# Layer 1 of a two-layer graph attention: weighted sums of h in 128x32 tiles, W applied to the sums, and scores from dot products on VectorE

## The chip, the cores and the metric

The kernel runs on one core of a Trainium2 chip. The metric is the device time of one execution in microseconds (us), the median of several runs; a profile of one execution shows what each engine does. TensorE multiplies matrices (PE in the profile; PEld are its weight loads), VectorE is DVE, ScalarE is ACT, GpSimd is POOL, and SP issues all DMAs here. Everything is float32 except masks.

## What is computed

There are 8 graphs (batches) of 2048 nodes with 256 features, and one adjacency matrix for all. Layer 0 is attention with four heads in which each chunk of 256 keys has a softmax of its own; then come a projection, a residual and two layer norms. Its result is h. Layer 1 is what the change touches:

```python
def _L1_gnn_ref(h, adj, W, a):
    Wh = jnp.einsum('bnf,fo->bno', h, W)
    a1 = a[:Fout, 0]
    a2 = a[Fout:, 0]
    s_i = Wh @ a1
    s_j = Wh @ a2
    e = jax.nn.leaky_relu(s_i[:, :, None] + s_j[:, None, :], negative_slope=LEAKY_ALPHA)   # 0.2
    mask = (adj > 0) | jnp.eye(N, dtype=bool)
    e = jnp.where(mask[None, :, :], e, -jnp.inf)
    attention = jax.nn.softmax(e, axis=-1)
    h_prime = jnp.einsum('bij,bjo->bio', attention, Wh)
    return jax.nn.elu(h_prime)

x = _layernorm(x + _L0_gnn_ref(x, adj, ...), axis=-1)      # this x is h
x = _layernorm(x + _L1_gnn_ref(x, adj, L1_gnn_W, L1_gnn_a), axis=-1)
```

h comes out of a layer norm without scale and offset, so its features sum to zero in each row.

## The kernel before

Work is cut into blocks of 512 queries (ib, four to a batch) and tiles of 128 keys. The order of instructions on every engine is that of the program: it is written out by hand in **beats**. A beat is one tile of 128 keys of layer 0 for one block of queries; a batch has 64 beats, all eight have 512, and a tail of shorter beats finishes layer 1.

In each beat layer 0 multiplies q and k into scores (L886, two heads side by side in 64x128 tiles), clips and masks them on VectorE (L897), exponentiates on ScalarE (L901), and for the pair of key tiles before multiplies with v and with ones (L955). This last is done in 128x32 tiles: four instructions, one per head, write four groups of 32 PSUM partitions, and each streams 512 columns; such a group of four is called a quad here. A float32 matmul is two instructions, so the profile counts each twice. The results are copied by ScalarE (un L963, ds L969), the sums go through DRAM (dc, rd, r), and VectorE and GpSimd scale and add them to ctxT (L990, L991).

A finished block of layer 0 goes through `fin` (L345): projection po (L361), residual, two layer norms, h stored to DRAM (L380), then h transposed on TensorE (pt, L387), copied (L388) and stored as hT_d (L392).

Layer 1 of a batch runs beside layer 0 of the next one. `prelude` (L479) loads hT in blocks, makes Wh and the two scores per node as columns of one product with W and two appended columns (pw, L402, copied at L403), lays s_j out as a row (sj_row), and finds for each query the largest s_j among its neighbours (`half_max`, L442, VectorE). Out of that `less_max` makes two rows per block, ab: s_i less the row maximum, and 0.2 s_i less the row maximum. The last batch has `last_prelude` (L521), in part in the tail.

A **step** of layer 1 is one tile of 128 keys for one block: 16 steps a block, 512 in all. Up to 1.5 start in a beat on average (1.3 in the last batch of layer 0, one in the tail). A step writes one tile w of 128x512, from a ring of five:

- `low` (L718, ScalarE): 0.2 s_j added to the second row of ab;
- `leaky` (L722, VectorE, one beat later): s_j added to the first row, and the larger of both;
- `edges` (L727, VectorE, middle of that beat): the smaller of this and a mask of 0 or -128;
- `weights` (L731, ScalarE, next beat): exp; and L740 (GpSimd) adds the tile to acc, for the row sums;
- `product` (L750, TensorE, end of that beat): four matmuls, each with 128 queries of w as weights and 256 columns of Wh streaming, into us (two PSUM banks).

In the last batch the row sum is a column of ones beside Wh (L765, 257 columns). After the sixteenth step ScalarE copies us to hx (L777); `fin1` (L592) sums acc over partitions with one-column matmuls (pr, L601), takes reciprocals, scales hx (L605), applies elu, adds h, normalizes and stores. `fin1_last` (L617) does this in smaller pieces.

The loops that issue all this are `begin_beat`, `middle_of_beat` and `end_beat` (L820 to L860) and the loop over beats (L904). Generators for side work (`fins`, `ahead`) advance once a beat, at its end, so a `yield` means one beat. Buffers come from pools named by their number of buffers; PSUM has ps_s (scores, two), ps_u (us, one) and ps_m (all else, two).

Of the kernel before, what the change touches and what calls it, by code (L numbers as in the profile page):

```python
# [14 lines left out]
ALU = mybir.AluOpType  # L15
# [13 lines left out]
def tile_adj_attention__then__gat(  # L29
# [16 lines left out]
    W: bass.AP,  # L46
    a: bass.AP,
# [43 lines left out]
    five = ctx.enter_context(tc.tile_pool(name="five", bufs=5))  # L91
# [26 lines left out]
    def xT_tile(b, ib, name):  # L118
        t = four.tile([P, KC, IB], F32, tag="xT", name=f"xT_{name}{b}_{ib}")
        nc.sync.dma_start(out=t, in_=xT[b, :, ts(ib, IB)].rearrange("(k p) n -> p k n", p=P))  # L120
        return t
# [104 lines left out]
    W_aug = const.tile([P, KC, F + 2], F32, name="W_aug")  # L226
    nc.sync.dma_start(out=W_aug[:, :, 0:F], in_=W.rearrange("(k p) o -> p k o", p=P))
    a_bc = []
    for n in range(2):
        t = one.tile([P, F], F32, tag=("hx", "ex")[n], name=f"a_bc{n}")  # L230
        nc.sync.dma_start(out=t, in_=a[n * F : (n + 1) * F, :].rearrange("f o -> (f o)").partition_broadcast(P))
        a_bc.append(t)

    def weights_made():

        for n in range(2):
            for k in range(KC):
                wa = one.tile([P, F], F32, tag="hr", name=f"wa{n}_{k}")
                nc.vector.tensor_mul(wa, W_aug[:, k, 0:F], a_bc[n])
                nc.vector.reduce_sum(W_aug[:, k, F + n : F + n + 1], wa, axis=AX.X)  # L240
            yield

        pb = ps_m.tile([P, F], F32, tag="m", name="pb")
        for k in range(KC):
            rep = one.tile([P, P], F32, tag=("hr", "ex")[k], name=f"bvr{k}")
            nc.vector.tensor_scalar(rep, ones, bv_c[:, k : k + 1], None, ALU.mult)
            nc.tensor.matmul(pb, rep, WT["o"][:, k, :], start=(k == 0), stop=(k == KC - 1))
        nc.vector.scalar_tensor_tensor(bo_bc, pb, float(NCH), bo_bc, ALU.mult, ALU.add)
# [91 lines left out]
    hT_d = dram.tile([B, NIB, P, KC, IB], F32, name="hT_d")  # L340
# [4 lines left out]
    def fin(b, ib, ctxT):  # L345
# [34 lines left out]
        nc.sync.dma_start(out=h_d[b, ib], in_=y)  # L380
        fin_near[b] += 1
        yield
        hT = four.tile([P, KC, IB], F32, tag="xT", name=f"hT{b}_{ib}")
        for k in range(KC):
            pt = ps_m.tile([P, TPB, P], F32, tag="m", name=f"pt{b}_{ib}_{k}")
            for t in range(TPB):
                nc.tensor.transpose(pt[:, t, :], y[:, t, ts(k, P)], ident)  # L387
            nc.scalar.copy(hT[:, k, :], pt.rearrange("p t c -> p (t c)"))  # L388
        if (b, ib) == (B - 1, NIB - 1):
            states[b]["hT"] = hT  # L390
        else:
            nc.sync.dma_start(out=hT_d[b, ib], in_=hT)  # L392

# [3 lines left out]
    def wh_block(b, wh, ht, ib):  # L397

        for t in range(TPB):
            pw = ps_m.tile([P, F + 2], F32, tag="m", name=f"pw{b}_{ib}_{t}")  # L400
            for k in range(KC):
                nc.tensor.matmul(pw, ht[:, k, ts(t, P)], W_aug[:, k, :], start=(k == 0), stop=(k == KC - 1))  # L402
            nc.scalar.copy(wh[:, t, :], pw)  # L403

    def load_hT(b, ib):
        t = four.tile([P, KC, IB], F32, tag="xT", name=f"hTl{b}_{ib}")
        nc.sync.dma_start(out=t, in_=hT_d[b, ib])
        return t

    def key_columns(wh, sj, r):  # L410

        nc.vector.tensor_copy(sj[:, 0, r], wh[:, :, F + 1])
        nc.vector.tensor_scalar_mul(sj[:, 1, r], wh[:, :, F + 1], SLOPE)
        nc.vector.tensor_copy(sj[:, 2, r], wh[:, :, F])
# [38 lines left out]
    def less_max(sj, ib, m2, name):  # L453
# [6 lines left out]
        nc.vector.tensor_sub(m2[:, 0, :], s_i, mx)  # L460
# [18 lines left out]
    def prelude(b):  # L479
# [5 lines left out]
        hts = [load_hT(b, ib) for ib in range(2)]  # L485
# [4 lines left out]
        wh = one.tile([P, NT, F + 2], F32, tag="wh", name=f"wh{b}")  # L490
        for ib in range(NIB):
            wh_block(b, wh[:, ts(ib, TPB), :], hts[ib], ib)
            if len(hts) < NIB:
                hts.append(load_hT(b, len(hts)))
            yield
        sj = two.tile([P, 3, NT], F32, tag="sj", name=f"sj{b}")
        key_columns(wh, sj, slice(0, NT))
        yield
        sj_row = one.tile([P, N], F32, tag="sj_row", name=f"sj_row{b}")
        key_rows(b, sj, sj_row, slice(0, NT))  # L500
        st["wh"], st["sj"] = [wh[:, ts(ib, TPB), :] for ib in range(NIB)], sj
        fbs, fb_load = far_loads(b, [(it, hf) for it in range(NT) for hf in range(2)])
        yield
        yield
# [16 lines left out]
    def last_prelude(b):  # L521
# [4 lines left out]
        wh, rows = [None] * NIB, [None] * 2  # L526
        halves = [slice(0, HT), slice(HT, NT)]
        sj = None
        for ib in range(NIB - 1):
# [3 lines left out]
            ht = load_hT(b, ib)  # L533
            yield
            yield
            wh[ib] = one.tile([P, TPB, F + 2], F32, tag=f"kT{ib}", name=f"wh{b}_{ib}")
            wh_block(b, wh[ib], ht, ib)
            if sj is None:
                sj = two.tile([P, 3, NT], F32, tag="sj", name=f"sj{b}")
            key_columns(wh[ib], sj, slice(ib * TPB, (ib + 1) * TPB))  # L540
            nc.vector.memset(wh[ib][:, :, F : F + 1], 1.0)
            yield
            if ib == 1:
                rows[0] = one.tile([P, HN], F32, tag="v0", name=f"sj_row{b}_0")
# [12 lines left out]
        while "hT" not in st:  # L557
# [11 lines left out]
        wh[-1] = one.tile([P, TPB, F + 2], F32, tag=f"kT{NIB - 1}", name=f"wh{b}_{NIB - 1}")  # L569
        wh_block(b, wh[-1], st["hT"], NIB - 1)  # L570
        key_columns(wh[-1], sj, slice(NT - TPB, NT))
        nc.vector.memset(wh[-1][:, :, F : F + 1], 1.0)
        rows[1] = one.tile([P, HN], F32, tag="v1", name=f"sj_row{b}_1")
        key_rows(b, sj, rows[1], halves[1])
        st["wh"], st["sj"] = wh, sj
# [16 lines left out]
    def fin1(b, ib, hx, acc):  # L592
# [3 lines left out]
        yield  # L596


        pr = ps_m.tile([P, TPB], F32, tag="m", name=f"pr{b}_{ib}")
        for t in range(TPB):  # L600
            nc.tensor.matmul(pr[:, t : t + 1], acc[:, ts(t, P)], ones[:, 0:1], start=True, stop=True)  # L601
        r = two.tile([P, TPB], F32, tag="r1", name=f"r1{b}_{ib}")
        nc.vector.reciprocal(r, pr)
        for t in range(TPB):
            nc.scalar.activation(hx[:, t, :], hx[:, t, :], AF.Identity, bias=ones[:, 0:1], scale=r[:, t : t + 1])  # L605
# [11 lines left out]
    def fin1_last(b, ib, hx):  # L617
# [9 lines left out]
        ends = ib == NIB - 1  # L627

# [65 lines left out]
    def layer1():  # L694

        for b in range(B):
            st = states[b]
            for ib in range(NIB):
# [3 lines left out]
                block = {"b": b, "ib": ib, "ab": st["ab"].pop(ib)[1], "wh": st["wh"], "sj": st["sj"], "mks": mks}  # L702
# [5 lines left out]
    class Step:  # L708
# [6 lines left out]
        def low(self):  # L715
            k, c = self.k, self.c
            self.w = five.tile([P, IB], F32, tag="w", name=f"w{self.name}")
            nc.scalar.activation(self.w, k["ab"][:, 1, :], AF.Identity, bias=k["sj"][:, 1, c : c + 1])  # L718

        def leaky(self):  # L720
            k, c = self.k, self.c
            nc.vector.scalar_tensor_tensor(  # L722
                self.w, k["ab"][:, 0, :], k["sj"][:, 0, c : c + 1], self.w, ALU.add, ALU.max
# [339 lines left out]
```

## Time and profile before

| | |
|---|---|
| median of three runs | 4353.48 us (4349.72 to 4354.51) |
| span of the profiled execution | 4356.1 us; its own device time is not listed, so the span stands for it |
| mean granted TensorE clock | 0.982 of full speed |
| first batch of layer 0 alone (0 to 411.6 us) | PE busy 381.5, DVE 289.0 |
| seven batches with layer 1 beside them (411.6 to 4085) | PE 3473.9 of 3673.4, DVE 2872.1, ACT 2171.6, POOL 1593.1 |
| tail (4085 to 4356) | PE 189.0 of 271.1, DVE 217.7, granted clock 0.87 |

Page and views have one line per group of instructions: line, engine, operation, what it writes and reads, shapes, count; then busy time and the mean of one in ns; then the idle time of that engine just before them and what ended it. The timeline has start, duration, engine, line and count, and merges neighbours of one kind; the end of a matmul is modelled, so a matmul's cost is best read from the start of the next one. A line of the windows view has the stretch, its length, each engine's busy time with its number of instructions, the granted TensorE clock, and the DMA engines' share and rate.

### The profile page before, as it was taken

The page shows a single profiled execution, that of the slowest core. Times are in us where ns is not written, and L with a number is a line of the kernel's source. Part 1 is how long each engine was busy: PE and PEld are TensorE (multiplying, and loading weights), DVE is VectorE, ACT ScalarE, POOL GpSimd, SP SyncE. Part 2 cuts the span into 40 slices and gives each one's busy share as a digit, 9 for nine tenths or more (in the row PEclk, how much of TensorE's full clock was granted, in tenths as well). Part 3 has the DMA queues.
Part 4 walks back from the last instruction along what each step waited for, and adds up shares of the span by engine and source line. Part 5 has one row for each costly group of instructions (what it writes and reads, how often), then busy time and mean ns, then how long its engine had stood idle before and what let it go on. Part 6 is the DMA issues. An engine that isn't in the chain of part 4 may idle for free.

```text
span 4356.1 us, 61109 instructions
## 1 busy us (share of the span) xinstructions
PE 4044.4 (93%) x23053; PEld 1915.6 (44%) x23053; DVE 3378.8 (78%) x4530; ACT 2556.2 (59%) x3842; POOL 1755.6 (40%) x901
## 2 busy tenths in 40 slices
PE   9899989999999999999899998999989999899767
PEld 3223334553345434444344543445434454344456
DVE  5875589865997768976699766996579965888777
ACT  5665556655666655666456665666555665555546
POOL 0332245542454424544245442554335543345520
PEclk9999999999999999999999999999999999999989
DMA  5554333213332133321333223232232222322321
GB/s 184 180 178 139 91 95 102 76 53 108 103 101 73 49 106 101 105 72 60 108 93 96 74 76 102 87 92 79 77 103 89 84 79 72 118 81 80 125 68 59
DMA packets 257641, 415.63 MB, mean 95 GB/s; under 512 B 85440, under 2 KB 120512, under 8 KB 256448
## 3 DMA queue, kind: packets, MB, share of 16 engines
q1 hardware_dynamic: 257344, 411.71, 30.9%
q8 instruction: 181, 2.97, 0.3%
q14 instruction: 116, 0.95, 0.1%
HBM read 340.66 MB, written 68.88 MB: 94 GB/s over the span
## 4 chain that ended last, share of the span: by engine, by line
PE 58%; DVE 22%; ACT 7%; DMA 6%; issue 5%; POOL 1%; SPq 0%; DVEq 0%; ACTq 0%; POOLq 0%
PE u L955 18%; PE sc L886 14%; PE us L750 12%; DVE sc L897 6%; DVE w L722 3%; DVE fb L442 3%; PE pk L256 3%; PE pv L275 3%; ACT e L901 2%; DMA dc<-ds 2%; PE po L361 2%; PE pq L256 2%; PE pw L402 2%; DVE w L727 2%; PE us L765 1%
## 5 line engine op out<-in xcount | busy, mean ns | idle before, releaser
L901 ACT ACTIVATE e<-sc 128x1024 f32<-128x1024 f32 x1024 | 1033.7, 1021 | 961.5 <-DVE sc L897 936.8
L897 DVE SCALAR_TENSOR_TENSOR sc<-sc,mk 128x1024 f32<-128x1024 f32 x1024 | 1205.5, 1222 | 503.9 <-PE sc L886 353.5
L886 PE MATMUL sc<-qT,kT 64*128 64x512 f32 x4096 | 1034.6, 621 | 45.2 <-ACT e L901 41.8
L991 POOL TENSOR_TENSOR ctxT<-ctxT,un 128x1024 f32<-128x1024 f32 x224 | 556.7, 2485 | 1247.9 <-DVE un L990 1220.3
L955 PE MATMUL u<-e,v 128*32 128x512 f32 x8192 | 979.4, 596 | 0.0
L750 PE MATMUL us<-wh,w 128*128 128x256 f32 x3584 | 880.6, 395 | 84.0 <-ACT w L731 62.5
L750 PEld LDWEIGHTS us<-wh,w 128*128 128x128 f32 x3584 | 667.5, 193 | 426.4 <-ACT w L731 114.7
L740 POOL TENSOR_TENSOR acc<-acc,w 128x512 f32<-128x512 f32 x392 | 599.5, 1529 | 548.3 <-ACT w L731 537.7
L722 DVE SCALAR_TENSOR_TENSOR w<-ab,sj,w 128x512 f32<-128x512 f32 x512 | 591.2, 1176 | 5.8 <-ACT w L718 5.8
L886 PEld LDWEIGHTS sc<-qT,kT 64*128 64x128 f32 x4096 | 345.5, 187 | 553.5 <-issue 310.0
L955 PEld LDWEIGHTS u<-e,v 128*32 128x32 f32 x8192 | 240.1, 109 | 655.3 <-issue 500.9
L955 PE MATMUL u<-e,ones 128*32 128x512 f32 x4096 | 492.5, 598 | 0.0
L727 DVE TENSOR_TENSOR w<-w,mk 128x512 f32<-128x512 f32 x512 | 441.4, 883 | 45.0 <-DMA mk<-mask 42.5
L442 DVE CUSTOM_DVE_ANT_0 fb<-sj_row,fb 128x1024 bf16<-128x1024 f32 x240 | 372.2, 1562 | 22.0 <-DMA fb<-far 22.0
L963 ACT COPY un<-u 128x512 f32<-128x512 f32 x512 | 300.8, 587 | 107.8 <-PE u L955 100.0
L718 ACT ACTIVATE w<-ab,sj 128x512 f32<-128x512 f32 x512 | 352.2, 714 | 10.7 <-POOL acc L738 5.5
L731 ACT ACTIVATE w<-w 128x512 f32<-128x512 f32 x512 | 308.8, 629 | 82.8 <-DVE w L727 82.4
L990 DVE TENSOR_TENSOR un<-un,r 128x1024 f32<-128x1024 f32 x224 | 279.7, 1249 | 45.5 <-DMA r<-rd 45.0
L955 PEld LDWEIGHTS u<-e,ones 128*32 128x32 f32 x4096 | 106.8, 109 | 346.9 <-issue 279.1
L977 DVE RECIPROCAL dc<-dc 128x16 f32<-128x16 f32 x256 | 63.6, 249 | 146.7 <-DMA dc<-ds 140.7
L361 PE MATMUL po<-WT_o,ctxT 128*128 128x256 f32 x512 | 133.9, 420 | 45.8 <-POOL ctxT L991 44.9
L969 ACT COPY ds<-u 128x512 f32<-128x512 f32 x256 | 148.5, 580 | 15.0 <-PE u L955 13.7
(112 smaller groups left out, 3064.2 us busy)
## 6 DMA issues: line engine op xcount, KB each, us to landing
r<-rd SPq DMA_DIRECT2D x256, 256.0 KB
mk<-mask SPq DMA_DIRECT2D x120, 512.0 KB
fb<-far SPq DMA_DIRECT2D x240, 256.0 KB
xT_k<-in_xT_dram SPq DMA_DIRECT2D x32, 512.0 KB
raw<-in_adjT_dram SPq DMA_DIRECT2D x32, 512.0 KB
rawf<-in_adj_dram SPq DMA_DIRECT2D x32, 512.0 KB
x<-in_x_dram SPq DMA_DIRECT2D x32, 512.0 KB
h_d<-y SPq DMA_DIRECT2D x32, 512.0 KB
```

The lines of the kernel that those rows point to most:

```text
L442: nc.vector.tensor_tensor_reduce(out=fb, in0=row, in1=fb, scale=1.0, scalar=2 * FAR * 0.999, op0=ALU.add, op1=ALU.max, accum_out=dst,)
L718: nc.scalar.activation(self.w, k["ab"][:, 1, :], AF.Identity, bias=k["sj"][:, 1, c : c + 1])
L722: nc.vector.scalar_tensor_tensor(self.w, k["ab"][:, 0, :], k["sj"][:, 0, c : c + 1], self.w, ALU.add, ALU.max)
L727: nc.vector.tensor_tensor(self.w, self.w, self.k["mks"][self.c // HT][:, self.c % HT, :], ALU.min)
L731: nc.scalar.activation(self.w, self.w, AF.Exp)
L740: nc.gpsimd.tensor_add(k["acc"], k["acc"], self.w)
L750: nc.tensor.matmul(k["us"][:, t, :], self.w[:, ts(t, P)], k["wh"][c // TPB][:, c % TPB, 0:F], start=(first and t % 2 == 0), stop=last, ski ...
L886: nc.tensor.matmul(sc[:, h, :], kTs[b][n // TPB][h * D : (h + 1) * D, hp, ts(n % TPB, P)], qTs[b, ib][h * D : (h + 1) * D, hp, :], start=True,
L897: nc.vector.scalar_tensor_tensor(sc, sc, -CLIP, cap, ALU.max, ALU.min)
L901: nc.scalar.activation(e, sc, AF.Exp)
L955: nc.tensor.matmul(m[h * DH : (h + 1) * DH, :], prev["v"][pc // TPB][:, pc % TPB, f0 : f0 + DH] if part < 2 else ones[:, 0:DH], prev["es"] ...
L991: nc.gpsimd.tensor_add(p["ctxT"], p["ctxT"], p["un"])
```

## The change

Since the features of h sum to zero, h W equals the sum over features 1 to 255 of h_f (W_f - W_0). So feature 0 of h can be overwritten by ones: layer 1 sums h itself, weighted, with a column of ones in place of feature 0, and W less its first row (W_less, whose own first row is zero) multiplies the sums afterwards. The row of ones gives the softmax's row sums.

- `fin` no longer transposes h. VectorE takes eight dot products per block (two per 128 nodes) of h with W a1 and W a2, which are made once.
- `prelude` loads h itself (255 columns, and ones by memset) where hT was loaded and Wh made, and it starts the row maxima before it waits for the batch before.
- `low` is gone: max(s_i + s_j, 0.2 (s_i + s_j)) is written as s_j + max(0.8 s_i, -0.8 s_j) + 0.2 s_i, so `leaky` takes a max with a column and adds a row, and `edges` adds s_j and takes the mask's minimum in one instruction. The ring of w has four tiles. GpSimd no longer adds acc.
- `product` takes h as weights (128 keys x 32 features, 8 matmuls a step in quads) and streams w, so the sums come out transposed: features on partitions, 512 queries in the columns.
- After the sixteenth step the sums are copied to agg; the row of sums goes through DRAM into columns (z_d, r), two beats later reciprocals are taken, W_less multiplies agg, and ScalarE scales out of PSUM. In the very last block the row sum is a 257th column of this product instead.

```diff
@@ fin @@
-        hT = four.tile([P, KC, IB], F32, tag="xT", name=f"hT{b}_{ib}")
-        for k in range(KC):
-            pt = ps_m.tile([P, TPB, P], F32, tag="m", name=f"pt{b}_{ib}_{k}")
-            for t in range(TPB):
-                nc.tensor.transpose(pt[:, t, :], y[:, t, ts(k, P)], ident)
-            nc.scalar.copy(hT[:, k, :], pt.rearrange("p t c -> p (t c)"))
...
+        for t in range(TPB):
+            if t % 2 == 0 and not last:
+                yield
+            c = ib * TPB + t
+            for n, slot in ((0, 2), (1, 0)):
+                nc.vector.tensor_tensor_reduce(
+                    out=dots, in0=y[:, t, :], in1=wa_bc[n], scale=1.0, scalar=0.0,
+                    op0=ALU.mult, op1=ALU.add, accum_out=sj[:, slot, c : c + 1],
+                )
...
+    def load_h(b, ib, hb):
+        nc.sync.dma_start(out=hb[:, :, 1:F], in_=h_d[b, ib][:, :, 1:F])
+        nc.vector.memset(hb[:, :, 0:1], 1.0)
@@ Step @@
-        def low(self):
-            self.w = five.tile([P, IB], F32, tag="w", name=f"w{self.name}")
-            nc.scalar.activation(self.w, k["ab"][:, 1, :], AF.Identity, bias=k["sj"][:, 1, c : c + 1])
...
+            self.w = four.tile([P, IB], F32, tag="w", name=f"w{self.name}")
             nc.vector.scalar_tensor_tensor(
-                self.w, k["ab"][:, 0, :], k["sj"][:, 0, c : c + 1], self.w, ALU.add, ALU.max
+                self.w, k["ab"][:, 0, :], k["sj"][:, 1, c : c + 1], k["ab"][:, 1, :], ALU.max, ALU.add
             )
...
-            nc.vector.tensor_tensor(self.w, self.w, self.k["mks"][self.c // HT][:, self.c % HT, :], ALU.min)
+            nc.vector.scalar_tensor_tensor(
+                self.w, self.w, k["sj"][:, 0, c : c + 1], k["mks"][c // HT][:, c % HT, :], ALU.add, ALU.min
+            )
...
-                nc.gpsimd.tensor_add(k["acc"], k["acc"], self.w)
...
+            for n in range(KC):
+                for g in range(H):
+                    f0 = n * P + g * DH
                     nc.tensor.matmul(
-                        k["us"][:, t, :],
-                        self.w[:, ts(t, P)],
-                        k["wh"][c // TPB][:, c % TPB, 0:F],
+                        k["us"][g * DH : (g + 1) * DH, n, :],
+                        k["hb"][c // TPB][:, c % TPB, f0 : f0 + DH],
+                        self.w,
...
+    def spread_sums(b, ib, agg, r):
+        z_d = dram3.tile([IB], F32, tag="z_d", name=f"z_d{b}_{ib}")
+        nc.sync.dma_start(out=z_d, in_=agg[0:1, 0, :])
+        nc.sync.dma_start(out=r, in_=z_d.rearrange("(t p) -> p t", p=P))
+        yield
+        yield
+        nc.vector.reciprocal(r, r)
+
+    def weighted_means(b, ib, agg, r, hx):
+        for t2 in range(TPB // 2):
+            pw = ps_m.tile([P, 2, F], F32, tag="m", name=f"pw{b}_{ib}_{t2}")
+            for j in range(2):
+                t = 2 * t2 + j
+                for k in range(KC):
+                    nc.tensor.matmul(
+                        pw[:, j, :], agg[:, k, ts(t, P)], W_less[:, k, 0:F], start=(k == 0), stop=(k == KC - 1)
+                    )
+                nc.scalar.activation(
+                    hx[:, t, :], pw[:, j, :], AF.Identity, bias=ones[:, 0:1], scale=r[:, t : t + 1]
+                )
```

## Prediction

> **What bounds the kernel now.** I read the page's busy times first, then the windows of one steady batch, then the timeline for the spacing of TensorE's work, then the waits and the tail.
>
> ```profile
> PE 4044.4 (93%) x23053; PEld 1915.6 (44%) x23053; DVE 3378.8 (78%) x4530; ACT 2556.2 (59%) x3842; POOL 1755.6 (40%) x901
> ...
> L750 PE MATMUL us<-wh,w 128*128 128x256 f32 x3584 | 880.6, 395 | 84.0 <-ACT w L731 62.5
> ...
> L740 POOL TENSOR_TENSOR acc<-acc,w 128x512 f32<-128x512 f32 x392 | 599.5, 1529 | 548.3 <-ACT w L731 537.7
> L722 DVE SCALAR_TENSOR_TENSOR w<-ab,sj,w 128x512 f32<-128x512 f32 x512 | 591.2, 1176 | 5.8 <-ACT w L718 5.8
> ...
> L718 ACT ACTIVATE w<-ab,sj 128x512 f32<-128x512 f32 x512 | 352.2, 714 | 10.7 <-POOL acc L738 5.5
> ```
>
> The next view is the busy time of each engine (PE, PEld, DVE, ACT, POOL) in two stretches of one batch: layer 1 beside the row maxima (L442), and layer 1 without them.
>
> ```profile
> 1120.00:1360.00 240.00, 226.61 (x1282) 111.56 (x1275) 225.34 (x281) 145.95 (x222) 124.13 (x64) 0.99 0.30 90
> 1360.00:1520.00 160.00, 159.66 (x895) 81.17 (x893) 108.05 (x143) 96.90 (x146) 71.25 (x41) 1.00 0.21 61
> ```
>
> In the second TensorE never rests (159.7 of 160 us); in the first TensorE and VectorE are both at 94%. ScalarE is far from full in either, so the 352 us of L718 are no gain by themselves. From 411.6 to 4085 us the windows give TensorE 3473.9 us of 3673.4. So what TensorE need not do there comes off the time almost one for one. The tail (4085 to 4356) is another regime: PE 189 of 271 us, DVE 218.
>
> The timeline's start-to-start spacing, not the modelled ends, is what a piece of TensorE work costs:
>
> ```profile
> 1302.18 1.99 PE L886 MATMUL sc<-qT,kT 64*128 64x512 f32 x8
> ...
> 1304.10 1.92 PE L955 MATMUL u<-e,ones 128*32 128x512 f32 x16
> ...
> 1305.84 1.90 PE L955 MATMUL u<-e,v 128*32 128x512 f32 x16
> ...
> 1307.67 1.99 PE L750 MATMUL us<-wh,w 128*128 128x256 f32 x8
> ...
> 1309.50 0.98 PE L601 MATMUL pr<-ones,acc 128*128 128x1 f32 x8
> ```
>
> Sixteen instructions in 128x32 tiles (four quads) followed by more of the same take 1.74 us (1304.10 to 1305.84); followed by 128x128 work 1.83. One step (x8) takes 1.83 when 128x128 work follows. Elsewhere in the timeline it takes 1.93 when scores follow (972.63 to 974.56), two steps and then scores take 3.67, and u followed by scores takes 1.83 to 1.86 (1059.24 to 1061.10).
>
> **The change, part by part.**
>
> *The product.* A step becomes 16 instructions in 128x32 tiles, the form of L955: I price it as L955, 1.74 us. One step, then scores: before u 1.84 + us 1.93 = 3.77; after u 1.74 + product 1.85 = 3.59, so -0.18. Two steps: 1.84 + 3.67 against 1.74 + 1.74 + 1.85, also -0.18. Where 128x128 work follows: 3.66 against 3.59, -0.07. In the built order of before, 297 such runs follow u, 161 of them ending at scores: 161 x 0.18 + 136 x 0.07 = **-38 us**. In the last batch 40 instructions of L765 (five steps) stand at 9.32 us, 1.86 a step; 64 x 0.12 = **-8 us**. Bounds: a quad at the 0.425 us by which weight loads follow each other inside a run of L955 gives -20 more; dearer quads are the rival below.
>
> *Transposes, row sums, Wh.* L387 goes (39.1 us, its busy time) and L601 goes (27.4 us): **-66 us**. pw stays as work: 512 instructions of L402 before, 512 after, moved from before layer 1 into the end of each block; no change on TensorE. Their waits: L387 lists 33.8 us idle before it and L402 10.9; pw in its new place waits for the same PSUM pair and for r, so I keep 28 of these 45: **-17 us** (0 to -45).
>
> *ScalarE.* L718 (352), the wh copies (48.1) and the hT copies (35.9) go; the activations that scale hx (L605, 589 ns) become PSUM reads (L784, 564); agg is copied as hx was (L777, 1.0 us). About -436 us on an engine at 59%: counted only through shorter waits.
>
> *VectorE.* L442 shows a product-and-reduce over 1024 elements at 1.22 us plus 0.08 for its accumulator; for the new dots (256 of them, 256 elements) no row exists. Between L319 (256 elements, 0.40) and L442 whole (1.30) I take 0.50, near L319, whose length it shares: +128 us (102 to 333), 4 us a block. The edges become a scalar_tensor_tensor with an int8 operand, between L727's least (0.672) and L722's least (0.650): 0. The other side is GpSimd: L722 runs from 650 to 2883 ns, mean 1176. In the tail:
>
> ```profile
> 4150.53 0.75 DVE L722 SCALAR_TENSOR_TENSOR w<-ab,sj,w 128x512 f32<-128x512 f32 x1
> ...
> 4178.50 1.46 POOL L740 TENSOR_TENSOR acc<-acc,w 128x512 f32<-128x512 f32 x1 [1.36 <-ACT w L731]
> 4178.76 1.74 DVE L722 SCALAR_TENSOR_TENSOR w<-ab,sj,w 128x512 f32<-128x512 f32 x1
> ```
>
> Started just behind an acc addition, L722 takes 1.0 us more. Over all rows the excess above their least is 269 us on L722, 108 on L727 and about 85 on L442, some 460 us; acc is 649 of GpSimd's 1756 us (37%), so about 170 us of it go. VectorE nets -40 us overall, and more than that where layer 1 runs, because the dots fall evenly and the acc excess does not. In the first window above, 42 of L722 took 55.0 us, 27 over their least: there VectorE goes from 94% to about 90% and sets the pace less often. Worth on the path: TensorE's waits for w (62.5, of which 34.7 in the tail), for e (41.8) and for ctxT (44.9); of about 115 us outside the tail I take a sixth: **-20 us** (+20 to -60).
>
> The Trainium skill speaks against the dots. SBUF — State Buffer, Who interferes with whom, says that a VectorE instruction with two SBUF inputs and a GpSimd one that reads SBUF exclude each other for a whole instruction, which the pair above agrees with; the dots have two such inputs. One meeting a block with L991 would be an estimated 32 x 2.3 = 74 us of VectorE.
>
> *What is queued behind the new waits.* The sum row goes through DRAM to columns (two small DMAs, one of 4-byte pieces). VectorE's reciprocal is two beats behind, some 15 us in the main part. The nearest chain is ds to dc (issue 4089.87, reciprocal at 4092.65) and sj to sj_row (4161.64 to 4166.28): 3 to 5 us, so it is covered there. On SP these two sit ahead of far, mask, rd and r issues, whose users are one or two beats off. In the tail beats last 2 to 3.5 us, the cover is gone and VectorE, then ScalarE and TensorE, wait some 2 us, four times: +8. The column of ones in hb waits on VectorE for the last product of the batch before; behind it stand row maxima, and seven times up to 2 us of VectorE's slack go. Four buffers of w instead of five: of two steps in a beat the second L722 waits for the end of the last beat's product, just before scores, whose clip could not start earlier; 0. Per block 512 KB less cross DMA, at a share of 0.2 to 0.4; 0.
>
> *Order.* In the built order layer 1 starts six beats sooner (batch 2: beat 212.5 for 218) and 73 instead of 80 steps stand behind layer 0's end: the seven cost about 1.74 each in the main part and give back about as much or more in the tail; 0.
>
> *Tail.* From y normalized (4150.5) to psj (4161.05) stand pt, pw, copies; after it eight dots and a multiply, 4 us: -6. Contention with acc gone: about 12 steps at -1.0: -12. Four means of 3.6 us on TensorE now lie in the tail, partly hidden: +10. The end copies agg and multiplies by W before the reciprocal: +3. With the +8 above: **+3 us**.
>
> Sum: -38 - 8 - 66 - 17 - 20 + 3 = -146. From the profiled span of 4356.1 us this is 4210; the median of the three runs, 4353.5, lies 2.6 lower, so **4207 us**.
>
> The skill has a rule against the product too. TensorEngine Tiling (Array Packing), Instruction Overhead, charges each matmul some 60 cycles; at the 2.4 GHz of TensorE: Matmul & The Clock Gate 4096 more instructions would be an estimated +102 us, and the sum 4309. The trace's sixteen in 1.74 us show no such charge beside eight in 1.74 (3.67 less 1.93), so I don't take it.
>
> **The rivals.**
> 1. *VectorE takes over* in the stretches with row maxima: dots at 1.30 and the remaining GpSimd work colliding more. For it: 94% there now. Against: the 27 us of excess in that window. Then those 240 of 529 us keep their length and 55% of the gain is left: 4275 us.
> 2. *Slower: the quads cost more than L955's.* All four tiles stream the same w and accumulate over 16 steps into two banks; L955 streams four tiles and accumulates over two. There are 512 x 4 = 2048 quads, at 435 ns; 71 ns more eat the gain, so it decides from 506 ns. At L955's whole mean of one, 596 ns, it is +330: 4537 us. Against it: L955's own accumulating half shows no slowdown in the even spacing.
> 3. *Nothing moves*, because the beat is set by layer 0's chain (scores, clip, exp, u): 4350 us. Against: no idle TensorE in the second window.
> 4. *More*: half of the 199 us that TensorE idles in the main part goes, and with it stretches at a lower granted clock (0.99 there, 0.87 in the tail): 4110 us.
>
> **How the numbers follow.** Forecast 0.62, rival 1 0.14, rival 2 0.08, rival 3 0.04, rival 4 0.12. The range reaches from rival 4's side to a little beyond rival 1, 4115 to 4290, and takes in the bounds of dots and waits; the two outermost cases stay out. Faster by over 0.2% (what a measurement of this kernel can tell from no change): 0.62 + 0.14 + 0.12 = 0.88; within 0.2%: 0.04; slower: 0.08.
>
> **What would show it.** Product rows at 16 instructions per 1.74 us and no wait of the u rows before them; leaky's mean falling from 1176 to about 900; dots near 0.42 + 0.08; DVE busy near 3320, ACT near 2120, POOL near 1106, PE near 3935. It is wrong if quads spread beyond 0.5 us, if VectorE is over 95% in the stretch with row maxima, if ScalarE or TensorE wait for the reciprocal of the sums in the main part, or if the tail grows beyond 271 us.

## The result, and the profile after

The changed kernel takes 4363.07 us (median; 4354.95 to 4371.12) against 4354.37 us (4349.72 to 4363.35) of the kernel before, run beside it: ratio 1.0020, 95% interval 1.0012 to 1.0029. The forecast was 4207. Some 9 us (0.2%) longer, then, where 146 us less were expected. The profiled execution has a span of 4369.2 us (before 4356.1), at a mean granted clock of 0.970 (before 0.982).

The first view is the page of the changed kernel: the busy times, then some groups. The third number of a group is the idle time of its engine just before it, with what ended most of that.

```profile
PE 3990.3 (91%) x26677; PEld 1350.9 (31%) x26677; DVE 3248.9 (74%) x5038; ACT 2192.0 (50%) x3153; POOL 1122.8 (26%) x481
...
L864 PE MATMUL sc<-qT,kT 64*128 64x512 f32 x4096 | 1048.8, 626 | 111.5 <-ACT e L879 111.5
L767 PE MATMUL us<-w,hb 128*32 128x512 f32 x8192 | 970.5, 608 | 96.4 <-ACT w L756 74.7
...
L745 DVE SCALAR_TENSOR_TENSOR w<-ab,sj 128x512 f32<-128x512 f32 x512 | 504.7, 1005 | 8.5 <-DMA ab<-ab_d 5.4
...
L751 DVE SCALAR_TENSOR_TENSOR w<-w,sj,mk 128x512 f32<-128x512 f32 x512 | 397.6, 798 | 87.6 <-DMA mk<-mask 85.3
...
L604 PE MATMUL pw<-W_less,agg 128*128 128x256 f32 x496 | 138.6, 414 | 53.6 <-ACT hx L607 50.2
L266 PE MATMUL pq<-xT_q,WT_q 128*128 128x512 f32 x248 | 135.2, 694 | 50.7 <-DMA xT_q<-in_xT_dram 39.9
```

Two rows of the page of before, for comparison:

```profile
L886 PE MATMUL sc<-qT,kT 64*128 64x512 f32 x4096 | 1034.6, 621 | 45.2 <-ACT e L901 41.8
...
L727 DVE TENSOR_TENSOR w<-w,mk 128x512 f32<-128x512 f32 x512 | 441.4, 883 | 45.0 <-DMA mk<-mask 42.5
```

All engines do less, and yet the span is no shorter: the idle column has grown. TensorE's waits for e ahead of the scores are 111.5 us (41.8 before), VectorE's for the mask 85.3 (42.5), and two rows carry waits that were nothing or next to it: pw for hx, pq for xT_q (39.9, before 1.8).

Next, the windows of the same two stretches of a batch, moved by that batch's start (columns as before):

```profile
1141.00:1381.00 240.00, 222.25 (x1555) 72.01 (x1551) 188.22 (x276) 118.35 (x173) 61.01 (x26) 0.97 0.26 80
1381.00:1541.00 160.00, 152.33 (x964) 58.77 (x960) 96.96 (x152) 82.86 (x121) 43.36 (x21) 0.99 0.18 55
```

TensorE now idles 17.8 of 240 us and 7.7 of 160, where it idled 13.4 and 0.3; VectorE has fallen from 94% to 78% in the first stretch. No engine has become the bound. And the clock fell from 0.99 to 0.97 in the first.

The timeline of TensorE gives the spacing of its work:

```profile
1299.06 1.92 PE L933 MATMUL u<-e,ones 128*32 128x512 f32 x16
1300.81 1.90 PE L933 MATMUL u<-e,v 128*32 128x512 f32 x16
1302.52 1.90 PE L767 MATMUL us<-w,hb 128*32 128x512 f32 x16
1304.35 1.99 PE L864 MATMUL sc<-qT,kT 64*128 64x512 f32 x8
```

u takes 1.71 to 1.75 us, the new product 1.83 ahead of the scores. The product costs what was forecast.

So the whole time is split by the trace's TensorE rows into three: TensorE idle; time at a granted clock of one half, which is charged with half of itself; and the rest, which is work. (A batch runs from its first scores to the next one's, the tail from the end of layer 0's last u; the last column is a kernel of the experiments.)

| us | before | changed | five repairs |
|---|---|---|---|
| seven batches: duration | 3683.1 | 3686.7 | 3502.3 |
| - TensorE idle | 199.5 | 257.3 | 126.5 |
| - at half clock | 75.1 | 157.0 | 64.9 |
| - rest (work) | 3446.1 | 3350.9 | 3343.4 |
| first batch: duration, idle, half clock, rest | 397.3, 24.3, 10.2, 367.8 | 407.5, 31.1, 23.9, 364.4 | 403.8, 30.3, 17.1, 365.0 |
| tail: the same | 261.4, 82.1, 70.3, 144.2 | 260.0, 84.8, 82.1, 134.2 | 253.1, 83.2, 71.0, 134.4 |

Work fell by 95.2 + 3.4 + 10.0 = 109 us. Idle time rose by 57.8 + 6.8 + 2.7 = 67, and half of the added half-clock time is 54: together +13 with the span's first microseconds, the difference of the two spans. The split charges half-clock time in which TensorE idles twice. Charged only where TensorE is busy, half-clock time rose by 80 us, which cost 40, and work fell by 95; the idle time is the same. So the work saved is 95 to 109 us, and the clock's part 40 to 54.

The timeline shows how idle time arises. Here are all engines at the start of a block; the mask of its first half is issued at 1267 us:

```profile
1267.31 0.94 SPq L140 DMA_DIRECT2D mk<-mask  x2
...
1273.59 1.90 PE L933 MATMUL u<-e,v 128*32 128x512 f32 x16
...
1275.58 0.75 DVE L751 SCALAR_TENSOR_TENSOR w<-w,sj,mk 128x512 f32<-128x512 f32 x1 [7.49 <-DMA mk<-mask]
...
1277.11 1.93 PE L767 MATMUL us<-w,hb 128*32 128x512 f32 x16 [1.61 <-ACT w L756]
...
1281.72 2.15 ACT L879 ACTIVATE e<-sc 128x1024 f32<-128x1024 f32 x2 [4.67 <-DVE sc L875]
...
1282.80 3.21 PE L864 MATMUL sc<-qT,kT 64*128 64x512 f32 x8 [3.77 <-ACT e L879]
```

`edges` (L751) needs the mask in the very beat in which it is issued, and holds VectorE for 7.5 us; behind it stand dots, row maxima and the next clips, so e is late and TensorE stands for 3.8 us. Then the clock: eight score instructions last 3.21 us in place of 1.99. Before, `low` took the beat in which the mask was issued, and `edges` came one beat later. The same block of the kernel before, 11.9 us from the issue to `edges` where it is now some 8, and no wait:

```profile
1284.70 0.72 ACT L718 ACTIVATE w<-ab,sj 128x512 f32<-128x512 f32 x1
...
1286.08 0.47 SPq L140 DMA_DIRECT2D mk<-mask  x1
...
1297.94 0.85 DVE L727 TENSOR_TENSOR w<-w,mk 128x512 f32<-128x512 f32 x1
```

### The profile page after: what moved, and what is told of

Same layout as the page of the kernel before. It is cut to its first block, busy times and chain, and to the rows that moved or that the text cites. A ratio compares the mean times of both kernels' runs of the same rounds, so it can differ in the third digit from the quotient of the medians.

```text
span 4369.2 us, 67831 instructions
## 1 busy us (share of the span) xinstructions
PE 3990.3 (91%) x26677; PEld 1350.9 (31%) x26677; DVE 3248.9 (74%) x5038; ACT 2192.0 (50%) x3153; POOL 1122.8 (26%) x481
## 4 chain that ended last, share of the span: by engine, by line
PE 59%; DVE 19%; DMA 9%; ACT 6%; issue 5%; SPq 1%; POOL 1%; DVEq 0%; ACTq 0%; POOLq 0%
PE u L933 18%; PE sc L864 14%; PE us L767 13%; DVE sc L875 6%; PE pw L604 3%; PE pq L266 3%; PE pk L266 3%; PE pv L285 3%; DVE w L745 3%; PE po L370 2%; DVE w L751 2%; DMA mk<-mask 2%; DVE fb L451 2%; DMA dc<-ds 2%; DMA rd<-dc 2%
## 5 line engine op out<-in xcount | busy, mean ns | idle before, releaser
L864 PE MATMUL sc<-qT,kT 64*128 64x512 f32 x4096 | 1048.8, 626 | 111.5 <-ACT e L879 111.5
L767 PE MATMUL us<-w,hb 128*32 128x512 f32 x8192 | 970.5, 608 | 96.4 <-ACT w L756 74.7
L745 DVE SCALAR_TENSOR_TENSOR w<-ab,sj 128x512 f32<-128x512 f32 x512 | 504.7, 1005 | 8.5 <-DMA ab<-ab_d 5.4
L767 PEld LDWEIGHTS us<-w,hb 128*32 128x32 f32 x8192 | 263.4, 112 | 743.8 <-issue 545.9
L751 DVE SCALAR_TENSOR_TENSOR w<-w,sj,mk 128x512 f32<-128x512 f32 x512 | 397.6, 798 | 87.6 <-DMA mk<-mask 85.3
L451 DVE CUSTOM_DVE_ANT_0 fb<-sj_row,fb 128x1024 bf16<-128x1024 f32 x240 | 343.4, 1441 | 52.1 <-DMA fb<-far 52.1
L623 POOL TENSOR_TENSOR hx<-hx,hr 128x1024 f32<-128x1024 f32 x28 | 88.5, 3159 | 425.4 <-DVE hx L622 425.4
L604 PE MATMUL pw<-W_less,agg 128*128 128x256 f32 x496 | 138.6, 414 | 53.6 <-ACT hx L607 50.2
L266 PE MATMUL pq<-xT_q,WT_q 128*128 128x512 f32 x248 | 135.2, 694 | 50.7 <-DMA xT_q<-in_xT_dram 39.9
L607 ACT ACTIVATE hx<-pw,ones,r 128x256 f32<-128x256 f32 x124 | 69.9, 563 | 172.3 <-PE pw L604 157.4
```

The lines of the kernel that those rows point to most:

```text
L266: nc.tensor.matmul(pm, WT[name][:, k, ts(o, P)], xt[:, k, :], start=(k == 0), stop=(k == KC - 1))
L451: nc.vector.tensor_tensor_reduce(out=fb, in0=row, in1=fb, scale=1.0, scalar=2 * FAR * 0.999, op0=ALU.add, op1=ALU.max, accum_out=dst,)
L745: nc.vector.scalar_tensor_tensor(self.w, k["ab"][:, 0, :], k["sj"][:, 1, c : c + 1], k["ab"][:, 1, :], ALU.max, ALU.add)
L751: nc.vector.scalar_tensor_tensor(self.w, self.w, k["sj"][:, 0, c : c + 1], k["mks"][c // HT][:, c % HT, :], ALU.add, ALU.min)
L767: nc.tensor.matmul(k["us"][g * DH : (g + 1) * DH, n, :], k["hb"][c // TPB][:, c % TPB, f0 : f0 + DH], self.w, start=first, stop=last,)
L864: nc.tensor.matmul(sc[:, h, :], kTs[b][n // TPB][h * D : (h + 1) * D, hp, ts(n % TPB, P)], qTs[b, ib][h * D : (h + 1) * D, hp, :], start=True,
```

## The experiments

Theory G: the work saved is real, and waits that the change makes give it back, with the half clock that follows them: the mask's lost lead, the queue behind z, the load of h, the order around pw (and, at first, the ring of xT). Rival L: layer 0's chain sets a beat whatever TensorE does. Rival W: the ring of w, four for five, stalls. All kernels were timed beside the kernel before. "us" below is the difference of two ratios times 4360; each ratio is uncertain by about 0.0013, so such a difference by some 8 us.

**One repair at a time.** The mask, loaded in step 11 of the block before:

```diff
-                while ib not in st["ab"] or beat < st["ab"][ib][0]:
+                while ib not in st["ab"]:
+                    yield None
+                if early is None:
+                    early = mask_block(1, ib, 0, f"{b}_{ib}_0")
+                while beat < st["ab"][ib][0]:
                     yield None
-                mks = [mask_block(1, ib, 0, f"{b}_{ib}_0")]
+                mks = [early]
...
+                    if c == 11 and (b, ib) != (B - 1, NIB - 1):
+                        early = mask_block(1, (ib + 1) % NIB, 0, f"{b}_{ib}_next")
```

> The changed kernel, with one thing moved: the first half of a block's mask is loaded in step 11 of the block before it, not in the beat of its first use. Theory G (the 95 us of TensorE work saved in the seven batches are real, and are given back by waits that the change makes: the mask's lost lead, the queue behind z, the load of h, the order around pw, and the half clock that follows gaps): VectorE's waits for mk fall from 85 us to under 15, TensorE's waits for e in front of sc from 102 to about 50, the time at half clock by some 40 us; the time falls by 45 to 75 us, to about 4305. Rival L (the chain of a layer-0 beat sets its length whatever TensorE does): the waits for mk fall too, and the time stays within 10 us of 4363, since the same idle time turns up as waits for ACT e at other beats. Rival W (four buffers of w in place of five are what stalls): within 10 us of 4363, and L745 shows waits for the release of w.

Measured: ratio 0.9856 (0.9840 to 0.9871), 72 us less than the changed kernel. VectorE's waits for mk, 85.3 us before the repair, are gone; in the seven batches idle fell by 44 and half-clock time by 51. G.

pw, with the matmuls of both tiles ahead of the activations:

```diff
         for j in range(2):
             t = 2 * t2 + j
             for k in range(KC):
                 nc.tensor.matmul(...)
+        for j in range(2):
+            t = 2 * t2 + j
             nc.scalar.activation(hx[:, t, :], pw[:, j, :], ...)
```

> The changed kernel, with the matmuls of both tiles of a pw in front of the two activations that read it. Theory G: the 37.7 us in which pw waits for hx (58 times about 0.65 us) go, the clock hardly changes as these gaps are short: 4363 falls by 25 to 38 us, to about 4332. Rival L: the beat that holds the pw gets shorter on TensorE and then waits for e: within 10 us of 4363. Rival W: within 10 us.

Measured: 0.9878 (0.9862 to 0.9895), 62 us less, where G had 25 to 38. The timelines show why. First the changed kernel, then this one:

```profile
1291.65 1.13 PE L604 MATMUL pw<-W_less,agg 128*128 128x256 f32 x4
1293.44 1.99 PE L604 MATMUL pw<-W_less,agg 128*128 128x256 f32 x8 [0.66 <-ACT hx L607]
1296.09 1.13 PE L604 MATMUL pw<-W_less,agg 128*128 128x256 f32 x4 [0.66 <-ACT hx L607]
1297.15 1.99 PE L864 MATMUL sc<-qT,kT 64*128 64x512 f32 x8
```

```profile
1286.86 3.72 PE L604 MATMUL pw<-W_less,agg 128*128 128x256 f32 x16
1290.51 1.99 PE L866 MATMUL sc<-qT,kT 64*128 64x512 f32 x8
```

ScalarE reads one half of a PSUM tile while TensorE wants to write the other half, and TensorE waits. The waits are listed with 1.3 us a block, but the block takes 5.50 us in place of 3.65: the ends of matmuls are modelled, and starts tell the cost. 31 blocks x 1.85 = 57 us.

h, loaded in four beats:

```diff
-        for ib in range(NIB):
-            load_h(b, ib, st["hb"][ib])
...
                 fb_load()
+                if ib == 0 and n % 2:
+                    load_h(b, n // 2, st["hb"][n // 2])
```

> The changed kernel, with the four loads of h of a batch (2 MB) issued in four beats, one each, and not in one. Theory G: the gaps at the start of a batch (3.8, 1.8 and 3.4 us of TensorE idle and 3.4 to 6.8 us at half clock behind them) go in six or seven batches: 27.2 us of waits for xT_q fall to under 8; the time falls by 30 to 60 us, to about 4320. Rival L: within 10 us of 4363. Rival W: within 10 us.

Measured: 0.9987 (0.9979 to 0.9996), 14 us less, below the range that G gave: TensorE's waits for xT_q fell from 27.2 to 11.4 us in the seven batches, but its idle time, all causes together, only by 11. VectorE's waits for far fell too, from 52.1 to 16.8 us (22.0 in the kernel before): the four loads had delayed these as well.

z, read one beat after it is written (`if b < B - 1: yield` between the two DMAs of `spread_sums`):

> The changed kernel, with the read of z issued one beat after its write (but in the last batch) and nothing else. Theory G: the queue's 73.2 us of waiting for z_d go, but the masks that stand behind it are still loaded in the beat of their first use, so VectorE's 85 us of waits for mk fall by 10 to 30 us only: the time falls by 5 to 25 us. Rival: the queue at z has slack, and the time stays within 5 us of 4363.

Measured: 0.9979 (0.9970 to 0.9988), 18 us less, in G's range, but not by its way: VectorE's waits for mk did not fall (89.2 us), but TensorE's for e did, from 101.6 to 87.2 us in the seven batches. The DMA queue's waits, changed kernel and then this one:

```profile
SPq L592 <- DMA z_d<-agg: 73.2, 31, 4.3
```

```profile
SPq L594 <- DMA z_d<-agg: 2.6, 3, 0.9
```

The ring of xT, four again (`four.tile` in `xT_tile`):

> The changed kernel with four buffers of xT again and nothing else. Theory R (the ring of three delays the loads of xT_q): the waits of pq for xT_q, 12.7 us in the first batch and 27.2 us in the others, fall to a third, and the time falls by 20 to 40 us. Theory C (in the first batch it is the transposes of the blocks of h that stood in front of pq and covered the load, and later the burst of h): the 12.7 us stay within 2 us, as they did with all five repairs (11.7 us), and the time falls by at most 10 us.

Measured: 1.0027 (1.0016 to 1.0038), no gain; the first batch's 12.7 us of waits are 14.3. The ring is not the cause. Theory C's cause is read from the timelines of the first batch: before, TensorE reached pq 5.4 us after the issue of xT_q, behind transposes of 1.9 us and their wait of 2.7 us; after, 1.1 us after it.

The ring of w, five again:

> The changed kernel with five buffers of w as before and nothing else. Theory G: within 8 us of 4363, since TensorE's idle time names w, e, hx, agg and xT_q and no step waits for a free w for long. Rival W: the time falls by 20 us or more.

Measured: 1.0030 (1.0018 to 1.0043), no gain. W falls.

**All five together** (mask, pw, h, z, xT):

> The changed kernel with all five repairs: mask a few steps ahead, pw's matmuls ahead of its activations, h in four beats, the read of z one beat after its write (but in the last batch), and four buffers of xT as before. Theory G: TensorE's idle time in the seven batches falls from 257 to about 150 us and its time at half clock from 157 to about 60: 4363 minus 105 minus 50 minus some 8 in the first batch gives 4200, at least under 4260. Rival L: over 4330, with TensorE's waits for e above 90 us. Rival W: over 4330, with waits on w.

Measured: 4179.15 us, 0.9593 (0.9580 to 0.9606): 186 us less than the changed kernel, 4% faster than the kernel before. The page, and a window of the same stretch of a batch as above:

```profile
PE 3929.0 (94%) x26677; PEld 1342.7 (32%) x26677; DVE 3246.0 (78%) x5038; ACT 2180.4 (52%) x3153; POOL 1129.5 (27%) x481
...
L875 PE MATMUL sc<-qT,kT 64*128 64x512 f32 x4096 | 1045.2, 623 | 80.5 <-ACT e L890 77.5
```

```profile
1116.00:1356.00 240.00, 235.06 (x1678) 81.08 (x1670) 196.63 (x295) 127.78 (x191) 68.87 (x28) 1.00 0.28 85
```

TensorE is busy 235 of 240 us and the clock is back at 1.00. None of the five touches the work, and the table above shows it within 8 us of the changed kernel's in the seven batches. L falls.

**One repair taken out of the five.**

> The kernel with the five repairs, with the mask's load put back into the beat of its first use. Theory S (each repair returns its own idle time, and they add up): 4179 rises by the 69 us that the mask's repair alone had brought, to about 4248. Theory J (a wait of VectorE for mk is dear only where ScalarE or the queue is late for other reasons in the same beats, as a late mask cost the kernel before only 9 us although VectorE's waits for mk doubled to 84.7 us): the rise is 5 to 30 us.

Measured: 0.9799 (0.9785 to 0.9812), 90 us more than with all five. Neither theory: it is 18 us more than the repair alone had brought (72), with an uncertainty of some 11. Half-clock time rises from 65 to 154 us, idle from 127 to 187.

> The kernel with the five repairs, with the old order around pw. Theory S: 4179 rises by the 62 us that this repair alone had brought, to about 4241. Theory T (only the 50 us of TensorE's waits for hx return, 37.7 in the seven batches and 12.5 in the tail; the rest of the 62 came from waits that are gone by now): the rise is 40 to 55 us.

Measured: 0.9714 (0.9699 to 0.9730), 53 us more. T's range, and what the starts gave (57).

> The kernel with the five repairs, with the four loads of h in one beat again. Theory S: 4179 rises by the 13 us that this repair alone had brought. Theory J (the start of a batch then has gaps over 2.5 us that no other late load hides, with 3.4 to 6.8 us of half clock behind each): the rise is 30 to 60 us.

Measured: 0.9642 (0.9629 to 0.9655), 21 us more: between S and J.

**How much of the mask is the lost beat.** The kernel before, with its load one beat later:

```diff
-                mks = [mask_block(1, ib, 0, f"{b}_{ib}_0")]
+                mks = {}
...
         def leaky(self):
+            if c == 0:
+                k["mks"][0] = mask_block(1, k["ib"], 0, f"{self.name}_0")
```

> The kernel before, with one thing moved the other way: the load of a block's first half of the mask is issued one beat later, in the beat of its first use, as in the changed kernel; nothing else differs. Theory G (it is the lost lead that costs): VectorE's waits for mk rise from 42.5 us to about 85, the half clock by some 30 us, and the time by 25 to 60 us, to about 4400. Rival M (the mask is late in the changed kernel because of the new loads of h and the queue at z, not for its lead): the time rises by under 15 us.

Measured: 1.0021 (1.0011 to 1.0030), 9 us more than before: the time of rival M with the waits of theory G (42.5 before):

```profile
DVE w L729 <- DMA mk<-mask: 84.7, 18, 7.7
```

> The kernel before with the mask's first half loaded in step 11 of the block before, the same edit that took 69 us off the changed kernel. Theory G (the changed kernel's mask waits are dear since its VectorE chain has lost slack to TensorE; before, a beat of lead and 7.4 us beats hid most): VectorE's 42.5 us of waits for mk go, the time falls by 0 to 20 us. Rival K (the repair is a gain of its own that has nothing to do with the change): the time falls by 45 us or more.

Measured: 0.9931 (0.9918 to 0.9943), 30 us less: between G and K. So a part of what the long lead brings was there to be had before the change. Against this kernel, which has the mask's repair too, the five repairs are 147 us less. Then the changed kernel with the lead of before:

```diff
-                while ib not in st["ab"] or beat < st["ab"][ib][0]:
+                while ib not in st["ab"] or (early is None and beat < st["ab"][ib][0] - 1):
+                    yield None
+                if early is None:
+                    early = mask_block(1, ib, 0, f"{b}_{ib}_0")
+                while beat < st["ab"][ib][0]:
                     yield None
-                mks = [mask_block(1, ib, 0, f"{b}_{ib}_0")]
+                mks, early = [early], None
...
+                    if c == 14 and ib + 1 < NIB:
+                        early = mask_block(1, ib + 1, 0, f"{b}_{ib}_next")
```

> The changed kernel with the lead of the first half of the mask as it was before: one beat ahead of the block's first step (one or two at a block boundary), not five steps. Theory P (the lost beat of lead is what costs): the time falls by 40 to 65 us of the 69 that the long lead brought, to about 4310. Theory Q (a mask one beat ahead is late as well, and what is new is only its price): it falls by less than 25 us.

Measured: 0.9877 (0.9864 to 0.9890), 62 us less: P, and M falls, as only the lead was given back. VectorE's waits for the mask are all but gone:

```profile
DVE w L758 <- DMA mk_next<-mask: 2.4, 2, 1.8
DVE w L758 <- DMA mk<-mask: 0.8, 2, 0.5
```

So the lost beat costs the changed kernel 62 us, and cost the kernel before 9 us for the same 85 us of VectorE's waits.

**Why it is dearer after the change.** Two ideas. First, that the removed TensorE work had covered the waits; it was put back as fill:

```diff
+        for k in range(KC):
+            pt = ps_m.tile([P, TPB, P], F32, tag="m", name=f"pt{b}_{ib}_{k}")
+            for t in range(TPB):
+                nc.tensor.transpose(pt[:, t, :], y[:, t, ts(k, P)], ident)
...
+        pr = ps_m.tile([P, TPB], F32, tag="m", name=f"pr{b}_{ib}")
+        for t in range(TPB):
+            nc.tensor.matmul(pr[:, t : t + 1], agg[:, 0, ts(t, P)], ones[:, 0:1], start=True, stop=True)
```

> The changed kernel with TensorE work put back that nobody uses: the 8 transposes of each block of layer 0 and 4 matmuls of one column for each block of layer 1, as before the change, some 68 us by their durations before; nothing waits for them. Theory C (this work had stood in time in which VectorE's chain was late; the change removed cover): the time rises by under 25 us. Rival A (the work is on the path and the waits are another matter): it rises by 50 to 75 us, to about 4430.

> The same fill in the kernel with the five repairs. Both theories: TensorE is the bound there (94 percent busy), so the fill's 68 us show nearly in full: 50 to 75 us above 4179, about 4240.

Measured: 1.0145 (1.0132 to 1.0158), 55 us above the changed kernel, and 0.9776 (0.9762 to 0.9790), 80 us above the five repairs (5 more than both theories had). C falls: work taken off TensorE was worth about its own length beside the waits too. (The filled transposes stand some beats later than those of before, in the first batch behind pq and not ahead of it; there the waits for xT_q stay, 11.5 us, and whether the transposes had covered that load is not tested by this.) Second, that layer 1's steps stand at other beats (`beat + 3` for `beat + 2` in `prelude`):

> The changed kernel with layer 1 of each batch but the last started one beat later against layer 0; nothing else differs. Theory F (the price of a late mask depends on what TensorE has to do in the beat it falls in: 3.6 us of a projection covered 3.9 us of waiting in the kernel before): the time moves by 20 us or more, either way, while VectorE's waits for mk stay at 70 to 95 us. Rival: it stays within 10 us of the changed kernel's.

Measured: 1.0018 (1.0009 to 1.0027), nothing, with 87.7 us of waits for mk. F, as far as one beat tests it, falls. The traces say where the price arises: in the kernel before, an earlier or later mask moves only TensorE's waits for w (15.4 us ahead, 32.7 late, in the seven batches), and those for e stay (31.9, 29.5); in the changed one it moves e (79.6 with a beat's lead, 101.6 without), w (24.5, 33.5) and agg (17.6, 21.5). VectorE's waits for the mask also stand elsewhere: before, at the first block of each batch (seven of 5.0 to 6.8 us; with the later load at the first and third), after the change mostly at the second and third. Why the clips are late after the change and were not before stays open; dots and row maxima behind `edges` on VectorE are a candidate that wasn't tried.

**Further repairs.** xT_q loaded two beats sooner (`NCH - 3 - sooner`), and at the batch's start sj_row, far and h issued behind r:

> The kernel with all five repairs and two further ones: xT_q is loaded two beats sooner, and at the start of a batch the broadcast of sj_row, the first loads of far and those of h are issued behind the read of r in their beat, not in front of it. Theory G: the waits of pq for xT_q (11.7 us in the first batch, 15.5 later) fall under 6 us, and the one large gap left in each batch (4.2 us, with 6.8 us at half clock behind it, seven times) goes: 4179 falls by 35 to 65 us, to about 4130. Rival L (from here on a layer-0 beat's chain sets its length): within 12 us of 4179.

Measured: 4177.11 us, 0.9571 (0.9558 to 0.9584), 10 us less than the five, far short of G's 35. The first batch shrinks by 12 us, but the seven batches grow by 15: VectorE's waits moved from r (39.4 with the five) to far (19.9):

```profile
DVE fb L451 <- DMA fb<-far: 64.8, 16, 7.5
DVE un L979 <- DMA r<-rd: 7.9, 8, 1.6
```

> The kernel with the five repairs, with xT_q loaded two beats sooner and nothing else. If in e9 this part was a gain (first batch 12 us shorter) and the new order at the batch's start a loss (seven batches 15 us longer), the time falls by 10 to 25 us below 4179, to about 4162. If the load only takes the place of another in the queue, it stays within 6 us of 4179.

Measured: 4173.80 us, 0.9574 (0.9561 to 0.9587), 8 us less, of the uncertainty's size. But the first batch lasts 397.0 us (403.8 with the five) and its waits for xT_q are gone: in that batch the load was late. In time the two are alike, some 4.3% below the kernel before, and the fastest kernels here.

## Why the prediction was wrong

The sum of what TensorE need not do was nearly right; what was costed at nothing was not. In the prediction's terms: -112 for work, measured -95 to -109; -37 for old waits, measured +67 for all idle time; and for the clock, which had no term, +40 to +54.

- **Product, transposes, row sums.** -38 - 8 - 66 = -112 forecast, -95 to -109 measured (the table's rest, with the two ways to charge the clock). Quads did not get dearer: rival 2 falls. The charge per matmul of the Trainium skill (TensorEngine Tiling (Array Packing), Instruction Overhead), which the prediction had not taken, does not show either: sixteen instructions ahead of the scores take 1.83 us, where eight took 1.93.
- **Dots and contention.** 0.50 us taken, 0.42 + 0.08 measured; L745 means 1005 ns (about 900 forecast); VectorE lost 130 us of work where 40 were taken. Rival 1 falls. The meeting of a dot with GpSimd, which the prediction took from the Trainium skill (SBUF — State Buffer, Who interferes with whom) and put at an estimated 74 us, did not happen: none of the 256 dots ran beside a GpSimd instruction, the longest took 0.43 us, and so no run here shows what such a meeting costs.
- **Old waits** (-17 and -20) went in part: in the seven batches ctxT ahead of po fell from 39.6 to 6.8 us, ds ahead of pt and pab from 44.6 to nothing, -77 in all. But of the three waits behind the -20 only ctxT fell; those for e rose from 33.2 to 101.6 us, those for w from 27.8 to 33.5. The sign of that term was wrong.
- **The mask: "On SP these two sit ahead of far, mask, rd and r issues, whose users are one or two beats off."** This is the step that failed first. With `low` gone, the mask's user is in the same beat: 62 us for the lost beat (e14), and 72 to 90 for the long lead (e1, e10). `low` was weighed only as ScalarE's work; it was also the mask's lead. The same sentence failed for z: its read holds the queue for z's landing, 18 us (e5).
- **"pw in its new place waits for the same PSUM pair and for r."** It waits for its own hx, between the halves of one tile: 53 to 62 us (e11, e2).
- **"Per block 512 KB less cross DMA ... 0", "Order ... 0".** Bytes were right, times not: four loads of h at once cost 14 to 21 us (e4, e12). And in the first batch transposes and their wait had stood ahead of pq: with them gone xT_q was late there, 12.7 us for 1.8; loaded sooner, that batch lasts 397.0 us again (e18). That the transposes were its cover is read from the timelines, not shown.
- **The clock** was no term of the sum, though rival 4 had it as a gain: it cost 40 to 54 us.
- **Four buffers of w, tail:** 0 and +3 forecast; e8 shows no gain from a fifth, and the tail is 1.4 us shorter.
- **Rival 3** had the time nearly right (4350), by luck, and the mechanism wrong: with the waits repaired and TensorE's work the same, the beats shorten, to a time 28 us below the forecast. That this comes near the forecast is luck in part: 30 us of it are the mask's long lead, a gain that the kernel before could have had as well (e13).
- **The signs of being wrong** that the prediction named would not have led to the cause: a quad takes 0.43 to 0.46 us, VectorE is at 78% where row maxima run, the tail lasts 260 us, and ScalarE waited for the reciprocal of the sums once in the main part (6.3 us, at 3876 us).

## What to carry to other kernels

A removed stage is also a delay that some load behind it may be living on: for each instruction that a step issues, DMAs included, set its issue against its first user in the new order. Price work that goes from the bound engine at its spacing, and then look at every place where its neighbours now come sooner: what they wait for is the new cost. And TensorE pays twice for a long gap: here nearly every idle gap over 2.5 us (57 of 64) came with a spell at half clock.

## What the runs showed of the hardware

TensorE's idle gaps in the seven batches of three kernels (before, changed, five repairs), and how many came with a half-clock spell, one that began in the gap or within 3.5 us of its end:

| gap, us | 0.5 to 1.5 | 1.5 to 2.5 | over 2.5 |
|---|---|---|---|
| gaps | 234 | 56 | 64 |
| with half clock | 4 | 8 | 57 |

These kernels' spells there last 3.4 us (43) or 6.8 us (22) at 0.50. So a gap of 3 us costs up to 4.7 or 6.4 us, an estimate: some spells begin in the gap, and what lies in it costs nothing more. The Trainium skill, TensorE: Matmul & The Clock Gate, Why this matters for your kernels, advises against idle gaps over some 3 us between bursts of matmuls; the traces agree (41 of the 42 gaps over 3 us came with half clock), but 16 of the 22 between 2.5 and 3 us did too.

A matmul into one half of a PSUM tile waited for ScalarE's read of the other half: 0.66 us listed, and 0.9 by the starts. The trace ties this wait to a semaphore that the program waits for; what the chip would do without it is not shown.
